# A kernel that picks weights by id: loading W2 for the first batches by id, and b2's rows by GpSimd

## The chip, the cores and the metric

The kernel runs on one core of one Trainium2 chip. A core has a matrix engine (TensorE, PE in the profile; its weight loads are shown as PEld), a vector engine (VectorE, DVE), a scalar engine (ScalarE, ACT), a general engine (GpSimd, POOL) and SyncE (SP), which here issues nearly all transfers. Data lie in HBM, in the on-chip memory SBUF, and in PSUM, eight banks that TensorE writes into. The metric is the device time of one execution in microseconds. The median of three runs of the kernel before is 303.18 us (303.14 to 303.38).

## The reference, cut to what matters

```python
w1 = W1[language_ids]                 # x: (128 batches, 128 rows, 512), ids: (128,)
w2 = W2[language_ids]                 # W1: (10, 512, 128), W2: (10, 128, 512)
h = einsum('bsh,bha->bsa', x, w1) + b1[language_ids][:, None, :]
h = relu(h)
adapted = einsum('bsa,bah->bsh', h, w2) + b2[language_ids][:, None, :]
y = x + adapted
normed = (y - mean(y)) * rsqrt(var(y) + 1e-5)
out = x + normed * gamma[language_ids][:, None, :] + beta[language_ids][:, None, :]
```

Every batch is a tile of 128 rows by 512 columns of fp32 (256 KB), and each uses the weights of its own id, one of ten. One batch's W1 is 256 KB, one batch's W2 is 256 KB, and the tables of all ids are 2.5 MB each.

## The kernel before, in words

For each batch b TensorE does three things: it transposes x in four blocks (`transpose_x`, L271), multiplies the transposed x by the batch's W1 (`down`, L294, eight pieces), and multiplies the result, after ReLU, by the batch's W2 (`up`, L311, two pieces). ScalarE copies the transposed x out of PSUM (`copy_xT`, L275), applies ReLU with b1 (`relu`, L302), sums the squares (`square`, L351) and finds the root (`deviation`, L361). VectorE adds x, or x + b2, to the product and sums the rows (`residual`, L328), subtracts the mean and multiplies by gamma (`scale`, L394), and multiplies by the reciprocal deviation and adds x + beta (`finish`, L403). GpSimd forms x + b2 (`add_b2`, L281) and x + beta (`add_beta`, L288).

For some batches GpSimd does not form x + b2. In `b2_by_matmul` batches a small product on TensorE (L310) adds b2's row into PSUM ahead of `up`; in `b2_by_vector` batches VectorE adds it (`vector_b2`, L321).

The order of the work is written out by hand. The function `keep` ties every instruction to the one issued before it on the same engine, so that each engine works through its list in the order of the program text; across engines, waits follow from the data. The main loop runs over i = 3 to 121 and does in iteration i, with b = i - 3: the transposes of batch i, `down` of i - 1, `up` of i - 2, the vector work of b and of the pair before it, and the additions of GpSimd for b + 2. Before it stands a start written out line by line, after it an end written out likewise. Results leave in pairs of batches (`store`, L407).

Buffers bound how far one engine may run ahead: x in four tiles of four batches (`xp`), the sums x + b2 in four (`rp`), the results in eight pairs (`op`), a batch's W1 in seven (`wp`), products in five PSUM banks (`p_y`).

W2 is held whole in SBUF (`load_w2`, L165; ids 0 to 2 first, 3 to 9 later). `up` picks its id's columns by an address known at run time, so the first `up` waits for all of W2. W1 comes in two ways. For the first `FIRST` = 17 batches `load_first` (L161) loads the id's W1 directly from HBM. For the rest, all of W1 is held in SBUF (`load_w1`, four loads of 640 KB, L103), and `stage_w1` (L262) on ScalarE copies the id's part into the batch's tile. For the same first batches (`EARLY`) the transposes take x in another column order. The end of the kernel loads three more W1 by id.

SP's queue issues, in this order: the ids, gamma's rows, x of batches 0 and 1, W2 of ids 0 to 2, then W1 by id and x of the next batches alternately, W2 of ids 3 to 9 after the fourth W1, the four parts of W1 among batches 13 to 16, and at last x of 18 and 19. Behind these stand the stores and the later loads of x, one megabyte each (`load_x`, L71): stores 0 and 1, x of batches 20 to 23, three stores, x of 24 to 27, and so on. A load by id can be issued only when the ids have arrived and have been clamped by VectorE.

Each row of beta, gamma and b2 (30 rows) is spread over all 128 partitions at the start, in one of two ways: `spread` (L229, L232) multiplies a one-hot column by the rows on TensorE and lets ScalarE copy the product; `shuffle_rows` (L247) lets VectorE copy it out of a tile that holds all rows in each group of 32 partitions (`four_copies`). Before, `spread` does thirteen rows and `shuffle_rows` seventeen. The additions of GpSimd wait for all ten rows of beta, or of b2, since they pick by a run-time address too.

Of the kernel before, what the change touches and what calls it, by code (L numbers as in the profile page):

```python
# [19 lines left out]
FIRST = 17  # L20
EARLY = 17
LATE = 17
U = 2


@with_exitstack
def cond_resid_kernel(ctx: ExitStack, tc: tile.TileContext, x, itok, W1, b1, W2, b2, gamma, beta, out):
# [29 lines left out]
    op = ctx.enter_context(tc.tile_pool(name="op", bufs=8))  # L57
# [31 lines left out]

    warm = const.tile([P, 1], FP, name="warm")  # L90
# [6 lines left out]
    load_part(0, 2)  # L97
    keep(nc.scalar.dma_start(out=b1r, in_=b1))
# [63 lines left out]

    def load_w2(lo, hi):
        dst = w2[:, lo * H : hi * H].rearrange("p (l h) -> p l h", l=hi - lo)
        keep(nc.sync.dma_start(out=dst, in_=W2[lo:hi].rearrange("l a h -> a l h")))  # L165

    load_w2(0, 3)
    load_first(0)
    load_first(1)
    load_part(2, 4)  # L170
    load_first(2)
    load_first(3)
    load_w2(3, L)
    xs[1] = xp.tile([P, G, H], FP, tag="x", name="x_1")
    load_part(4, 6)
    load_first(4)
    load_first(5)
    load_part(6, 8)
    load_first(6)
    load_first(7)  # L180
    xs[2] = xp.tile([P, G, H], FP, tag="x", name="x_2")
    load_part(8, 10)
    load_first(8)
    load_first(9)
    load_part(10, 12)
    load_first(10)
    load_first(11)
    xs[3] = xp.tile([P, G, H], FP, tag="x", name="x_3")
    load_part(12, 14)
    load_first(12)  # L190
    load_w1(0)
    load_first(13)
    load_part(14, 16)
    load_first(14)
    load_w1(1)
    load_first(15)
    xs[4] = xp.tile([P, G, H], FP, tag="x", name="x_4")
    load_part(16, 18)
    load_w1(2)
    load_w1(3)  # L200
    load_first(16)
    load_part(18, 20)
# [20 lines left out]
    b2_b = const.tile([P, L * H], FP, name="b2_b")  # L223

    def spread(r, copier):
# [7 lines left out]
        else:  # L233
            keep(nc.vector.tensor_copy(dst, row))

# [17 lines left out]
    def b2_by_matmul(b):  # L253
        return b in (0, 1) or b >= B - 2

    def b2_by_vector(b):
        return b in (2, 3, 9, 13, 17, 21) or 24 <= b < B - 8 and (b % 16 in (1, 6, 11) or b % 32 == 30)
# [46 lines left out]
    def up(b):  # L304
# [6 lines left out]
        keep(nc.tensor.matmul(ys[b], lhsT=hT[b], rhs=w2[:, bass.ds(v * H, H)], start=not m, stop=True))  # L311
# [230 lines left out]
    spread(10, nc.scalar)  # L542
    spin(1, H)
    x_turn(0)
    transpose_b1()
    spread(11, nc.scalar)
    for n in (0, G):
        lid(n, ET.PE)
    shuffle_rows(0, 10)
    x_turn(1)  # L550
    spread(12, nc.scalar)
    spread(13, nc.scalar)
    down(0)
    relu(0)
    spread(14, nc.scalar)
    x_turn(2)
    spread(15, nc.scalar)
    down(1)
    relu(1)
    spread(16, nc.scalar)  # L560
    spread(17, nc.scalar)
    x_turn(3)
    down(2)
    relu(2)
    spread(18, nc.scalar)
    spread(19, nc.scalar)
    add_beta(0)
    add_beta(1)
    spread(20, nc.scalar)
    spread(21, nc.scalar)  # L570
    down(3)
    relu(3)
    spread(22, nc.scalar)
    add_beta(2)
    add_beta(3)
# [253 lines left out]
```

## Time and profile before

| what | value |
|---|---|
| median of three runs | 303.18 us |
| the profiled execution | 303.08 us, its span 301.3 us |
| TensorE busy | 293.5 us (97%) |
| VectorE busy | 294.0 us (98%) |
| ScalarE busy | 278.5 us (92%) |
| GpSimd busy | 281.0 us (93%) |
| transfers | 78.11 MB, mean 259 GB/s |

The profile is a record of one execution. Its page lists the busy time of each engine, the span in 40 slices with the busy share of engines and of transfers in tenths, the chain of work that ended last, the costliest groups of instructions, and the transfers by the line that issues them. Further views are answers from the same trace: the instructions of one engine in order of time, the busy time and the bytes in chosen stretches, the waits by pairs, and the time from the issue of a load to its landing. Names such as `py<-w,hT` read "written tile <- read tiles"; a row that ends in brackets tells how long the engine was idle before it and what ended that. A busy matrix engine is not one at its peak: its pieces overlap, so the distance between two starts says more than the length of a piece.

### The profile page before, as it was taken

The page shows a single profiled execution, that of the slowest core. Times are in us where ns is not written, and L with a number is a line of the kernel's source. Part 1 is how long each engine was busy: PE and PEld are TensorE (multiplying, and loading weights), DVE is VectorE, ACT ScalarE, POOL GpSimd, SP SyncE. Part 2 cuts the span into 40 slices and gives each one's busy share as a digit, 9 for nine tenths or more (in the row PEclk, how much of TensorE's full clock was granted, in tenths as well). Part 3 has the DMA queues.
Part 4 walks back from the last instruction along what each step waited for, and adds up shares of the span by engine and source line. Part 5 has one row for each costly group of instructions (what it writes and reads, how often), then busy time and mean ns, then how long its engine had stood idle before and what let it go on. Part 6 is the DMA issues. An engine that isn't in the chain of part 4 may idle for free.

```text
span 301.3 us, 7022 instructions
## 1 busy us (share of the span) xinstructions
PE 293.5 (97%) x1827; PEld 219.1 (73%) x1827; DVE 294.0 (98%) x785; ACT 278.5 (92%) x770; POOL 281.0 (93%) x236
## 2 busy tenths in 40 slices
PE   7899999999999999999999999999999999999993
PEld 3758787777777777777777777777777777777761
DVE  6989999999999999999999999999999999999996
ACT  5868789999999999999999999999999999999983
POOL 1299998999999999999999999999999999999982
PEclk9999999999999999999999999999999999999999
DMA  6999999996667776766687666668765767782826
GB/s 234 377 390 367 346 321 396 405 337 209 234 229 256 280 235 197 252 242 233 240 281 250 209 209 246 257 231 281 263 204 196 254 232 253 278 271 79 280 89 228
DMA packets 45353, 78.11 MB, mean 259 GB/s; under 512 B 2137, under 2 KB 9316, under 8 KB 45314
## 3 DMA queue, kind: packets, MB, share of 16 engines
q1 hardware_dynamic: 45254, 77.62, 74.9%
q8 instruction: 15, 0.25, 0.3%
q14 instruction: 24, 0.20, 0.2%
q10 hardware_dynamic: 60, 0.05, 0.1%
HBM read 44.11 MB, written 33.55 MB: 258 GB/s over the span
## 4 chain that ended last, share of the span: by engine, by line
PE 87%; DVE 5%; DMA 3%; issue 2%; SPq 1%; POOL 0%; DVEq 0%; POOLq 0%
PE ph L294 35%; PE py L311 35%; PE pxT L271 18%; DMA w<-in_L_cond_W_dram 3%; DVE py L328 1%; DVE o L488 1%; DVE py L394 1%; SPq L161 1%; DVE n L494 0%; SPq L143 0%; DVE rstd_of L370 0%; SPq L88 0%; DVEq L824 0%; DVE part_of L367 0%; DVE shift L434 0%
## 5 line engine op out<-in xcount | busy, mean ns | idle before, releaser
L288 POOL TENSOR_TENSOR o<-x,beta_b 128x512 f32<-128x512 f32 x121 | 158.4, 1331 | 12.8 <-DVE beta_b L247 11.6
L294 PE MATMUL ph<-xT,w1s 128*128 128x128 f32 x1024 | 135.4, 275 | 0.1
L311 PE MATMUL py<-w,hT 128*128 x256 | 131.5, 595 | 0.6 <-DMA w<-in_L_cond_W_dram 0.6
L294 PEld LDWEIGHTS ph<-xT,w1s 128*128 128x128 f32 x1024 | 124.9, 192 | 1.8 <-issue 0.8
L281 POOL TENSOR_TENSOR r<-x,b_b 128x512 f32<-128x512 f32 x92 | 122.7, 1334 | 0.0
L271 PEld LDWEIGHTS pxT<-ident,x 128*128 128x128 f32 x512 | 65.8, 149 | 66.3 <-issue 49.9
L394 DVE SCALAR_TENSOR_TENSOR py<-py,nmean,gamma_b 128x512 f32<-128x512 f32 x124 | 93.2, 752 | 0.0
L403 DVE SCALAR_TENSOR_TENSOR o<-py,rstd,o 128x512 f32<-128x512 f32 x116 | 86.5, 745 | 0.0
L351 ACT ACTIVATE sq<-py,sum 128x512 f32<-128x512 f32 x124 | 85.8, 692 | 0.2 <-DVE rstd L370 0.2
L275 ACT COPY xT<-pxT 128x512 f32<-128x512 f32 x128 | 74.7, 584 | 5.9 <-PE pxT L271 5.8
L271 PE MATMUL pxT<-ident,x 128*128 128x128 f32 x512 | 77.6, 274 | 0.9 <-ACT gamma_b L232 0.7
L328 DVE SCALAR_TENSOR_TENSOR py<-py,r 128x512 f32<-128x512 f32 x97 | 66.7, 688 | 0.1
L262 ACT COPY w1s<-w 128x512 f32 x108 | 66.2, 613 | 0.0
L302 ACT ACTIVATE hT<-ph,b1T 128x128 f32<-128x128 f32 x128 | 46.9, 367 | 8.6 <-PE ph L294 4.0
L311 PEld LDWEIGHTS py<-w,hT 128*128 128x128 f32 x256 | 39.0, 192 | 2.2 <-DMA w<-in_L_cond_W_dram 1.1
L351 ACT ACTIVATION_READ_ACCUMULATOR sq<-py,sum 128x1 f32 x124 | 25.1, 203 | 0.0
L328 DVE SCALAR_TENSOR_TENSOR py<-py,x 128x512 f32<-128x512 f32 x31 | 21.7, 699 | 0.8 <-PE py L311 0.3
L321 DVE TENSOR_TENSOR py<-py,b_b 128x512 f32<-128x512 f32 x27 | 18.6, 689 | 0.8 <-ACT xT L275 0.6
L361 ACT ACTIVATE root<-ssq,eps 128x2 f32<-128x2 f32 x62 | 16.4, 265 | 0.0
L328 DVE DVE_READ_ACCUMULATOR py<-py,r 128x1 f32 x97 | 13.4, 138 | 0.0
L342 ACT ACTIVATE nmean<-sum 128x2 f32<-128x2 f32 x61 | 12.1, 199 | 0.0
L370 DVE SCALAR_TENSOR_TENSOR rstd<-part,root 128x2 f32<-128x2 f32 x62 | 9.2, 149 | 0.0
(73 smaller groups left out, 104.5 us busy)
## 6 DMA issues: line engine op xcount, KB each, us to landing
out_dram<-o SPq DMA_DIRECT2D x62, 512.0 KB, 3.5
x<-in_x_dram SPq DMA_DIRECT2D x27, 1024.0 KB, 6.5
x<-in_x_dram SPq DMA_DIRECT2D x10, 512.0 KB, 6.0
w1s<-in_L_cond_W_dram SPq DMA_DIRECT2D x20, 256.0 KB, 7.7
w<-in_L_cond_W_dram SPq DMA_DIRECT2D x4, 640.0 KB, 8.4
w<-in_L_cond_W_dram SPq DMA_DIRECT2D x1, 1792.0 KB, 10.2
w<-in_L_cond_W_dram SPq DMA_DIRECT2D x1, 768.0 KB, 5.2
out_dram<-o SPq DMA_DIRECT2D x4, 128.0 KB, 1.7
```

The lines of the kernel that those rows point to most:

```text
L262: keep(nc.scalar.copy(w1s[b].rearrange("p k a -> p (k a)"), src))
L271: keep(nc.tensor.transpose(pxs[b][:, k, :], cols, ident))
L275: keep(nc.scalar.copy(xT[b], pxs.pop(b)))
L281: keep(nc.gpsimd.tensor_tensor(rs[b], xb(b), b2_b[:, bass.ds(v * H, H)], ALU.add))
L288: keep(nc.gpsimd.tensor_tensor(os[g][:, j, :], xb(b), beta_b[:, bass.ds(v * H, H)], ALU.add))
L294: nc.tensor.matmul(phs[b], lhsT=w1s[b][:, k, :], rhs=xT[b][:, k, :], start=(k == 0), stop=(k == KC - 1))
L302: keep(nc.scalar.activation(hT[b], phs.pop(b), AF.Relu, bias=b1T[:, bass.ds(lid(b, ET.Activation), 1)]))
L311: keep(nc.tensor.matmul(ys[b], lhsT=hT[b], rhs=w2[:, bass.ds(v * H, H)], start=not m, stop=True))
L328: nc.vector.scalar_tensor_tensor(ys[b], ys[b], 1.0, r, ALU.mult, ALU.add, accum_out=col(sums, b))
L351: nc.scalar.activation(sq, ys[b], AF.Square, bias=col(sums, b), scale=-float(H), accum_out=col(ssqs, b))
L394: nc.vector.scalar_tensor_tensor(ys[b], ys[b], col(nmeans, b), gamma_b[:, bass.ds(v * H, H)], ALU.add, ALU.mult)
L403: nc.vector.scalar_tensor_tensor(o, ys[b], rstds[g][:, j : j + 1], o, ALU.mult, ALU.add)
```

## The change

The transfers at the start are put into a new order. W2 of the first five batches is loaded by id into tiles taken from the result buffers (`load_early`), that of batch 0 as the first load by id; all of W2 comes later, in one load, behind x of batch 7. x of batches 2 to 9 comes batch by batch. W1 is loaded by id for eighteen batches instead of seventeen, and its last two parts stand behind x of 19. The load of batches 20 to 23 stands behind one store instead of two. b2 (20 KB) is loaded once more, as one row, by ScalarE's queue, and GpSimd spreads it over the partitions in two instructions. Of beta and gamma seven rows are spread by TensorE and thirteen shuffled by VectorE, in another order, and `up` of batch 0 now stands ahead of `down` of batch 3. b2 goes in by TensorE for batches 0, 1, 2 and 4, by VectorE for 3, 5, 8, 15, 17 and 23 among the first 24. There are nine output buffers instead of eight. The main loop's arithmetic stays the same.

```diff
-FIRST = 17
-EARLY = 17
-LATE = 17
+FIRST = 18
+EARLY = 18
+LATE = 18
+SOON = 5
...
-    op = ctx.enter_context(tc.tile_pool(name="op", bufs=8))
+    op = ctx.enter_context(tc.tile_pool(name="op", bufs=9))
...
+    keep(nc.scalar.dma_start(out=b2_b[0:1, :], in_=b2.rearrange("(o l) h -> o (l h)", o=1)))
...
+    def early_w2(b):
+        if b // 2 not in soon:
+            soon[b // 2] = op.tile([P, 2, H], FP, tag="o", name=f"soon_{b // 2}")
+        return soon[b // 2][:, b % 2, :]
+
+    def load_early(b):
+        src = W2[bass.ds(lid(b, ET.SP), 1)].rearrange("o a h -> a (o h)")
+        keep(nc.sync.dma_start(out=early_w2(b), in_=src))
...
-    load_w2(0, 3)
+    load_early(0)
     load_first(0)
+    load_part(2, 3)
+    load_early(1)
+    load_part(3, 4)
+    load_early(2)
     load_first(1)
-    load_part(2, 4)
     load_first(2)
     load_first(3)
-    load_w2(3, L)
...
-    load_part(4, 6)
+    load_part(4, 5)
     load_first(4)
     load_first(5)
-    load_part(6, 8)
+    load_early(3)
+    load_part(5, 6)
     load_first(6)
+    load_early(4)
+    load_part(6, 7)
     load_first(7)
+    load_part(7, 8)
+    load_w2(0, 10)
...
     load_part(16, 18)
+    load_w1(1)
+    load_part(18, 20)
+    load_first(16)
     load_w1(2)
     load_w1(3)
-    load_first(16)
-    load_part(18, 20)
+    load_first(17)
...
+    for half in range(2):
+        cols = slice(half * (L // 2) * H, (half + 1) * (L // 2) * H)
+        keep(nc.gpsimd.partition_broadcast(b2_b[:, cols], b2_b[0:1, cols]))
...
-        return b in (0, 1) or b >= B - 2
+        return b in (0, 1, 2, 4) or b >= B - 2
...
-        return b in (2, 3, 9, 13, 17, 21) or 24 <= b < B - 8 and (b % 16 in (1, 6, 11) or b % 32 == 30)
+        return b in (3, 5, 8, 15, 17, 23) or 24 <= b < B - 8 and (b % 16 in (1, 6, 11) or b % 32 == 30)
...
+        rhs = early_w2(b) if b < SOON else w2[:, bass.ds(v * H, H)]
+        keep(nc.tensor.matmul(ys[b], lhsT=hT[b], rhs=rhs, start=not m, stop=True))
...
-        if b == 8 or b > 12 and b % G == 2 and b // G + 3 < NG:
-            load_x(5 if b == 8 else b // G + 3)
-        up_to = i
+        if b == 6 or b > 12 and b % G == 2 and b // G + 3 < NG:
+            load_x(5 if b == 6 else b // G + 3)
+        up_to = 5 if i == 4 else i
```

The new start, between the first row spread and the main loop, reads:

```python
    spread(4, nc.scalar)
    x_turn(0)
...
    spin(1, H)
    x_turn(1)
    spread(18, nc.scalar)
...
    down(0)
    relu(0)
    x_turn(2)
    down(1)
    relu(1)
    spread(5, nc.scalar)
    spread(6, nc.scalar)
    shuffle_rows(2, 3)
    down(2)
    relu(2)
    x_turn(3)
...
    spread(1, nc.scalar)
    up(0)
    down(3)
    relu(3)
...
    spread(7, nc.scalar)
    x_turn(4)
    add_beta(0)
    add_beta(1)
...
    add_beta(2)
    up(1)
    add_beta(3)
```

63 lines of the change are left out of this document (31 added, 32 removed).

## The prediction

> **What bounds the kernel now.** I read the page first (busy times, the slices, the chain), then the order of time of TensorE, then the waits, then the loads.
>
> ```profile
> span 301.3 us, 7022 instructions
> PE 293.5 (97%) x1827; PEld 219.1 (73%) x1827; DVE 294.0 (98%) x785; ACT 278.5 (92%) x770; POOL 281.0 (93%) x236
> DMA  6999999996667776766687666668765767782826
> PE 87%; DVE 5%; DMA 3%; issue 2%; SPq 1%; POOL 0%; DVEq 0%; POOLq 0%
> PE ph L294 35%; PE py L311 35%; PE pxT L271 18%; DMA w<-in_L_cond_W_dram 3%; DVE py L328 1%; DVE o L488 1%; DVE py L394 1%; SPq L161 1%; DVE n L494 0%; SPq L143 0%; DVE rstd_of L370 0%; SPq L88 0%; DVEq L824 0%; DVE part_of L367 0%; DVE shift L434 0%
> ```
>
> All four engines are nearly full, but the chain is TensorE's: three groups of its matmuls make 88% of the span, and the only transfer in it is a load of W2 at the start. The DMA row matters as much: the transfer engines are full for the first nine of 40 slices (68 us), then half idle. A change of loads acts there.
>
> The order of time of TensorE (start, length, line, operation, what ended the idle time):
>
> ```profile
> 16.43 1.12 PE L311 MATMUL py<-w,hT 128*128 x2 [0.58 <-DMA w<-in_L_cond_W_dram]
> 22.17 0.63 PE L271 MATMUL pxT<-ident,x 128*128 128x128 f32 x4
> 25.75 1.02 PE L311 MATMUL py<-w,hT 128*128 x2
> 26.61 0.63 PE L271 MATMUL pxT<-ident,x 128*128 128x128 f32 x4
> 48.78 0.60 PE L271 MATMUL pxT<-ident,x 128*128 128x128 f32 x4
> 49.22 1.06 PE L294 MATMUL ph<-xT,w1s 128*128 128x128 f32 x8
> 50.97 0.60 PE L271 MATMUL pxT<-ident,x 128*128 128x128 f32 x4
> 53.16 0.60 PE L271 MATMUL pxT<-ident,x 128*128 128x128 f32 x4
> 279.21 0.60 PE L271 MATMUL pxT<-ident,x 128*128 128x128 f32 x4
> ```
>
> The rows of L271 are the transposes of batches 6 (22.17), 8 (26.61), 18 (48.78), 19 (50.97), 20 (53.16) and 123 (279.21). From 48.78 to 279.21 lie 105 batches: 2.19 us each. Two neighbours give 2.19 too, so TensorE goes back to back in a fixed pitch and never catches up. Whatever its position is at batch 20 or so is carried to the end, as long as the others follow. The kernel's time is therefore decided in the first 55 us: by TensorE's own work there, and by the loads that it waits for. The row at 16.43 is the start's only wait on a load: up(0) on the second W2 load.
>
> **The loads.** TensorE's three kinds of input come over SP's queue in the order in which they are issued. Columns below: stretch, its length, busy times, clock, DMA share, GB/s; then issues of SP, and time to landing of four of them (the load of W2's last seven ids at 6.22, W1 of batch 4 at 7.86, W1 of batch 16 at 37.63, the second store at 41.55).
>
> ```profile
> 0.00:4.00 4.00, 2.99 (x7) 0.88 (x7) 2.49 (x11) 1.91 (x3) 0.88 (x8) 1.00 0.33 110
> 4.00:16.00 12.00, 10.28 (x66) 7.57 (x65) 10.97 (x33) 9.92 (x22) 2.90 (x3) 1.00 1.03 378
> 16.00:24.00 8.00, 7.57 (x39) 5.01 (x40) 6.83 (x20) 5.24 (x17) 8.00 (x7) 1.00 1.05 388
> 24.00:32.00 8.00, 8.00 (x53) 6.35 (x52) 8.00 (x22) 6.50 (x20) 8.00 (x8) 1.00 1.09 359
> 32.00:40.00 8.00, 8.00 (x51) 6.11 (x50) 7.83 (x22) 6.48 (x19) 8.00 (x7) 1.00 1.12 334
> 40.00:48.00 8.00, 8.00 (x56) 6.53 (x55) 8.00 (x22) 6.50 (x20) 6.83 (x7) 1.00 1.09 350
> 48.00:52.00 4.00, 4.00 (x27) 2.95 (x27) 4.00 (x14) 3.91 (x12) 4.00 (x4) 1.00 1.05 398
> ...
> 1.52 0.41 SPq L88 DMA_DIRECT2D x<-in_x_dram  x1
> 1.98 0.47 SPq L165 DMA_DIRECT2D w<-in_L_cond_W_dram  x1
> 3.75 0.91 SPq L161 DMA_DIRECT2D w1s<-in_L_cond_W_dram  x2
> 37.63 2.82 SPq L161 DMA_DIRECT2D w1s<-in_L_cond_W_dram  x1
> 41.03 0.92 SPq L407 DMA_DIRECT2D out_dram<-o  x2
> 42.05 1.33 SPq L71 DMA_DIRECT2D x<-in_x_dram  x1
> ...
> DMA to landing us min/median/max: 10.2/10.2/10.2
> DMA to landing us min/median/max: 10.6/10.6/10.6
> DMA to landing us min/median/max: 7.1/7.1/7.1
> ```
>
> The share is above 1 from 4 us on: the engines have no gap to take more. Summing GB/s times length, the bytes moved stand at 0.44 MB at 4 us, 4.98 at 16, 8.08 at 24, 10.95 at 32, 13.62 at 40, 16.42 at 48, 18.01 at 52. I count the queue in units of 256 KB (0.262 MB: one batch's x, W1 or W2) and add 0.09 MB of rows. W2's second load ends at 18 units of queue, 4.8 MB: moved at 15.5, landed at 6.22 + 10.2 = 16.4, a lag of 0.9. Batch 4's W1: 5.6 MB, 17.5, landed 18.5, lag 1.0. Batch 16's W1 (55 units): 14.5 MB, 42.5, landed 44.7, lag 2.2. The second store (61 units): 16.1 MB, 47.1, landed 48.6 (the third row's 7.1 holds for both), lag 1.5. So a transfer lands when its place in the queue has been moved, plus 0.9 early, plus about 1.6 (0.9 to 2.2) later.
>
> **The change part by part.**
>
> *TensorE's start.* Thirteen row spreads become seven, two more b2 products are added (batches 2 and 4), up(0) needs only its own 256 KB. In the order of time, two adjacent pieces start 0.21 apart:
>
> ```profile
> 4.99 0.38 PE L229 MATMUL row<-parts,pick 96*128 96x512 bf16 x1
> 5.21 0.38 PE L529 MATMUL idle<-ones 128*128 128x512 bf16 x1
> 10.04 0.72 PE L271 MATMUL pxT<-ident,x 128*128 128x128 f32 x4 [0.71 <-ACT gamma_b L232]
> ```
>
> Six spreads less save 1.3, two products cost 0.4; the waits of 0.58 (W2) and 0.71 (a copy of a spread row) can go. Sum before batch 8: up to -2.1 us. VectorE (17 shuffled rows become 13) and ScalarE (13 copies become 7) get lighter and hide behind TensorE; ScalarE's one more DMA issue (about as long as SP's above, 0.4 us) stands ahead of its first work and is covered by the wait for batch 1's W1, now seventh of the units behind x0 and x1.
>
> *The same start by the loads.* The queue has now, ahead of the whole W2 load's end, x of batches 0 to 7 (8 units), early W2 (5), W1 of 0 to 7 (8), W2 (10): 31 units, 8.2 MB. By the stretches that is moved at 24.4. Before, W2's first load at 1.98 fed the engines until W1 could be addressed at 3.75; now nothing stands between x (0.61 MB with the rows, moved at about 4.45) and that 3.75. From x's issue at 1.52 to bytes in number (0.44 MB by 4 us) I estimate 1 us of latency, so bytes again from 4.75: 0.3 later. Landed: 24.4 + 0.3 + 0.9 = 25.6. up(5), the first product to need it, stood at 25.75. So of the 2.1 us hardly 0.1 is left at batch 5: the load of W2 takes the place of the work. Late next is x of batch 20.
>
> *The loads behind it.* Up to the end of load_x(5) (batches 20 to 23, one 1 MB load) the queue held 65 units, 17.1 MB: moved at 48 + (17.1 - 16.42)/0.398 = 49.8, landed with the lag of 1.6 at 51.4; TensorE wanted it at 53.16, 1.8 later. After: five W2 units and one W1 unit more, one store (2 units) less ahead of it: 4 units, 1.05 MB, and 0.02 for b2's row. At the 398 GB/s of that stretch 2.7 us (3.2 at 334). Landing: 51.4 + 2.7 + 0.3 = 54.4, TensorE's place 53.16: 1.2 us late. The second place says the same: W1 of batch 17 now comes from HBM behind all of W1, at 63 units, 16.6 MB, moved at 48.5, landed at 48.5 + 0.3 + 1.6 = 50.4; down(17) stood at 49.22: also 1.2. These two are one shift, not two: a TensorE that is 1.2 late at 17 meets batch 20's x in time. load_x(6) follows with one store less between: no later place is tight, since from 68 us on the engines have room.
>
> *ScalarE's W1 copy* moves from batch 17 to 18, one copy of 0.61 us less, and the pitch later; it waits for all of W1, which lands one unit ahead of batch 17's W1, about 49.7, where the copy would stand at 46.20 + 2.19 = 48.4. The wait falls into the same shift.
>
> ```profile
> 46.20 0.61 ACT L262 COPY w1s<-w 128x512 f32 x1
> ```
>
> *GpSimd.* It had no idle time but these two, and its result is used with a lead:
>
> ```profile
> 13.10 4.98 POOL L288 TENSOR_TENSOR o<-x,beta_b 128x512 f32<-128x512 f32 x4 [11.64 <-DVE beta_b L247]
> 18.03 1.28 POOL L281 TENSOR_TENSOR r<-x,b_b 128x512 f32<-128x512 f32 x1
> 47.58 2.51 POOL L288 TENSOR_TENSOR o<-x,beta_b 128x512 f32<-128x512 f32 x2 [1.17 <-DMA out_dram<-o]
> 209.01 1.38 POOL L281 TENSOR_TENSOR r<-x,b_b 128x512 f32<-128x512 f32 x1
> 213.67 0.68 DVE L328 SCALAR_TENSOR_TENSOR py<-py,r 128x512 f32<-128x512 f32 x1
> ```
>
> The smallest lead that I found: the sum done at 210.39, read at 213.67, 3.3 us. The trace has no partition broadcast. From below: four additions go in 4.93 us, so 1.23 for 512 columns is the engine's two-input pace; a one-input write could be three times as fast, 4 us for 5120 columns; from above: that pace itself, 12.3 us. From b2's row at about 4 us it ends at 8 to 16; I take 12, the middle, since neither row is nearer. The first addition waits also for the last beta row, which ScalarE now copies after relu(3): by TensorE's order about 16. So it starts at 16 instead of 13.1; two b2 additions less give 2.5 back: 0.4 behind before, with 3.3 of lead. Cost 0. If the cover goes, it costs what exceeds a start at 13.1 + 2.5 + 3.3 = 18.9. The ninth output buffer moves the wait of 1.17 to batch 18, where store 0, also about 4 us later, lets it stand at about 0.6: 0. A shift of TensorE by 1.2 adds as much lead.
>
> The Trainium skill, GPSIMD Engine Reference, section Instruction dispatch, says that the first call to a freshly loaded kernel pays about 6 us that no instruction shows. If the broadcast is such a call, by that estimate its range of ends becomes 14 to 22, of which only the upper part passes 18.9; no run here shows it yet.
>
> Sum on the profiled execution's 303.08 (span 301.3 and 1.8 around it; the median of the runs, 303.18, is 0.1 above): TensorE's work -2.1, taken back by W2's landing +2.0, then the later loads +1.3: **304.3 us**. Its own range is 303.4 (lag 0.9) to 305.8 (lag 2.2, 3.2 us for the units).
>
> **The rivals.**
> *The loads are hidden anyway.* Batch 20's x had 1.8 us to spare; if the lag shrinks to 0.9 because smaller transfers keep the 16 engines closer together, landing is 53.7 less what the engines gain, and TensorE stays within 0.5 of its old place: 303.2. For it: the lag of early loads. Against it: shares above 1 throughout.
> *Faster.* W2 lands a microsecond earlier than the sum (24.6), as it would if the 31 units went at the best stretch's 398 GB/s from 4.75 on with a lag below 0.9, and batch 17's W1 and batch 20's x follow as early: TensorE keeps 1.1 of its 2.1 and the time is 302.0. It decides from landings under 48.6 and 52.5 there. Against it: 1.05 MB more has to go through a full queue. The whole 2.1 (301.0) would need W2 by 23.6, when 8.2 MB have not been moved.
> *GpSimd becomes the bound.* A broadcast that ends at 21 starts the additions 2.1 past 18.9; its row of idle times shows no gap in which it could catch up: 305.2, at 24 us 308. For it: no row of this operation exists here; against: the rows' bounds end at 16. By the Trainium skill's rule above the upper bound would be 22.
> *The early batches alone do not gain,* W2's landing slipping to 26.5 with a lag as later: 303.8, then the same late loads. This is in the first case's range.
>
> **How the numbers follow.** The late loads, 0.55; hidden, 0.22; faster, 0.15; GpSimd, 0.08. The likeliest gives 304.3. A measurement of this kernel can tell about 0.2% (0.6 us) from no change. Faster by that: 0.15. Slower: GpSimd's 0.08 and of the late loads all but their lowest part, 0.51: 0.59. Within: 0.26. The range leaves out the lower half of the faster case and the tails of GpSimd's and of the late loads: 302.1 to 305.6.
>
> **What would show it.** Right: the waits of TensorE name W2 at L338 near 25 to 26, and near 49 to 54 W1 of batch 17 or x, 1 us or more; the transposes of batch 20 begin at 54.4, from there the pitch is 2.19; additions on GpSimd begin near 16. Wrong: batch 20's transposes before 52.6 (the queue moved more than 400 GB/s, or the lag fell), a wait of VectorE for GpSimd (broadcast too long), or a pitch other than 2.19 after 60 us, which would make the start no measure of the end.

## The result, and the profile after

The changed kernel takes 311.88 us (median; 310.98 to 313.05), the kernel before 303.28 us on the same chip (303.14 to 303.40): a ratio of 1.0292, 95% interval 1.0275 to 1.0310. It is slower by 8.6 us; 304.3 was forecast, with a range to 305.6. The profiled execution took 310.98 us, its span 309.2 us, 7.9 us over the span of 301.3 before.

The page of the changed kernel: span, busy time of two engines, the share of the transfer engines by slice, the chain of work that ended last.

```profile
span 309.2 us, 7035 instructions
PE 295.9 (96%) x1823; PEld 220.9 (71%) x1823; DVE 291.5 (94%) x777; ACT 275.9 (89%) x763; POOL 284.2 (92%) x236
DMA  5999999998766766886767667887667668872825
PE 72%; DVE 13%; issue 7%; DMA 5%; SPq 1%; DVEq 1%; POOL 0%; POOLq 0%
```

TensorE has four matmuls fewer, and 2.4 us more busy time (1.7 of it by the half clock below); VectorE and ScalarE have less work. Most of the 7.9 us lies in waits. TensorE in order of time, changed kernel (start, length, line, operation, idle time before it and what ended that):

```profile
12.73 1.13 PE L320 MATMUL ph<-xT,w1s 128*128 128x128 f32 x8 [2.35 <-DMA w1s<-in_L_cond_W_dram]
16.23 1.02 PE L338 MATMUL py<-soon,hT 128*128 128x512 f32 x2
28.74 1.10 PE L338 MATMUL py<-w,hT 128*128 x2 [1.73 <-DVE o L430]
29.68 0.63 PE L297 MATMUL pxT<-ident,x 128*128 128x128 f32 x4
51.88 0.60 PE L297 MATMUL pxT<-ident,x 128*128 128x128 f32 x4
58.72 0.63 PE L297 MATMUL pxT<-ident,x 128*128 128x128 f32 x4 [2.30 <-DMA x<-in_x_dram]
59.18 1.57 PE L320 MATMUL ph<-xT,w1s 128*128 128x128 f32 x8
60.55 1.91 PE L338 MATMUL py<-w,hT 128*128 x2
62.25 0.95 PE L297 MATMUL pxT<-ident,x 128*128 128x128 f32 x4
227.22 0.60 PE L297 MATMUL pxT<-ident,x 128*128 128x128 f32 x4
```

The rows of L297 are the transposes of batches 8 (29.68), 18 (51.88), 20 (58.72), 21 (62.25) and 96 (227.22). Before, batches 8, 18 and 20 began at 26.61, 48.78 and 53.16: the lateness is 3.07, 3.10 and 5.56. Batches 21 and 22 add the rest, to 7.25, and from there it stands: 7.29 at batch 96 by the row at 219.93 below. The first step is the product of batch 5 at 28.74. The row puts its wait down to VectorE, but the trace's record of W2's one load shows its last part landed at 28.61, and in x5_parts below, which has the same start, the same product began at 27.23, right behind W2's landing at 27.09 and ahead of the same VectorE instruction, which it therefore does not need. The second is the x of batch 20. The third is not a wait: behind 58.72 the pieces are half as long again. The stretches (length, busy times, granted clock, share of the transfer engines, GB/s), changed kernel:

```profile
4.00:6.00 2.00, 1.16 (x4) 0.60 (x4) 1.06 (x2) 0.93 (x2) 0.00 (x0) 1.00 0.52 184
6.00:11.00 5.00, 4.38 (x25) 3.23 (x23) 4.17 (x14) 3.53 (x7) 2.60 (x1) 1.00 1.00 313
48.00:52.00 4.00, 4.00 (x27) 3.00 (x26) 3.88 (x10) 3.28 (x10) 4.00 (x4) 1.00 1.04 314
52.00:56.00 4.00, 4.00 (x29) 3.06 (x27) 3.94 (x11) 3.84 (x13) 4.00 (x5) 1.00 0.90 307
56.00:59.56 3.56, 1.26 (x9) 0.87 (x9) 3.56 (x10) 1.40 (x5) 3.56 (x3) 1.00 1.04 403
59.56:62.97 3.41, 3.41 (x13) 2.26 (x12) 0.50 (x2) 2.26 (x7) 3.41 (x4) 0.50 1.05 407
```

In the last row the clock is 0.50 for 3.41 us, which costs 1.7 us. The first two rows matter against the same stretches of the kernel before:

```profile
4.00:6.00 2.00, 1.40 (x9) 0.94 (x8) 1.25 (x2) 1.28 (x3) 0.00 (x0) 1.00 1.04 354
6.00:11.00 5.00, 4.03 (x25) 2.83 (x25) 4.72 (x17) 3.63 (x8) 0.00 (x0) 1.00 1.03 382
```

By 11 us the changed kernel has moved 2 x 170 + 5 x 69 = 685 KB less, 1.8 us of transfers at the 382 GB/s of the last row.

GpSimd, changed kernel, in order of time, and then the instructions of its lines L260 and L314 (length in ns min/median/max, first and last start):

```profile
8.40 5.48 POOL L260 PARTITION_BROADCAST b_b<-b_b  x2 [6.71 <-issue]
22.58 7.42 POOL L314 TENSOR_TENSOR o<-x,beta_b 128x512 f32<-128x512 f32 x6 [8.70 <-ACT nmean L369]
292.74 2.51 POOL L450 TENSOR_TENSOR o<-x,beta_b 128x512 f32<-128x512 f32 x2
```

```profile
L260 POOLq MODIFY_POOL_CONFIG  x2: 11/11/11, 1.7 to 1.7; - x2
...
L314 POOLq MODIFY_POOL_CONFIG  x2: 127/127/127, 13.8 to 13.8; - x2
```

GpSimd is told to change its configuration at 1.7, the broadcast begins 6.7 us later; it is told to change back at 13.8, and the first addition begins 8.8 us later, at 22.58 instead of 13.10. Of the 9.5 us in between, a part is the new order of the start: ScalarE's copy of the last beta row now ends at 19.02 (begun at 18.44, 0.58 long). From the kernel before, as the mark for the far end of the run, TensorE's transposes of batch 96 and GpSimd's last pair of beta additions:

```profile
219.93 0.60 PE L271 MATMUL pxT<-ident,x 128*128 128x128 f32 x4
```

```profile
286.66 2.61 POOL L423 TENSOR_TENSOR o<-x,beta_b 128x512 f32<-128x512 f32 x2
```

So at the far end TensorE is 7.29 us late and GpSimd 292.74 - 286.66 = 6.08 us. In this profiled execution, the fastest of the four, TensorE is the later of the two, and the chain of the page names GpSimd with 0%. The other three executions have no profile.

### The profile page after: what moved, and what is told of

Same layout as the page of the kernel before. It is cut to its first block, busy times and chain, and to the rows that moved or that the text cites. A ratio compares the mean times of both kernels' runs of the same rounds, so it can differ in the third digit from the quotient of the medians.

```text
span 309.2 us, 7035 instructions
## 1 busy us (share of the span) xinstructions
PE 295.9 (96%) x1823; PEld 220.9 (71%) x1823; DVE 291.5 (94%) x777; ACT 275.9 (89%) x763; POOL 284.2 (92%) x236
## 4 chain that ended last, share of the span: by engine, by line
PE 72%; DVE 13%; issue 7%; DMA 5%; SPq 1%; DVEq 1%; POOL 0%; POOLq 0%
PE ph L320 29%; PE py L338 28%; PE pxT L297 14%; DVE py L355 4%; DVE py L421 4%; DMA x<-in_x_dram 3%; DMA w1s<-in_L_cond_W_dram 2%; DVE o L430 2%; DVE o L515 1%; DVE py L348 1%; DVE part L394 0%; DVE n L521 0%; SPq L175 0%; DVE part L392 0%; PE row L251 0%
## 5 line engine op out<-in xcount | busy, mean ns | idle before, releaser
L314 POOL TENSOR_TENSOR o<-x,beta_b 128x512 f32<-128x512 f32 x121 | 155.6, 1302 | 8.7 <-ACT nmean L369 8.7
L338 PE MATMUL py<-w,hT 128*128 x246 | 127.3, 599 | 1.7 <-DVE o L430 1.7
L307 POOL TENSOR_TENSOR r<-x,b_b 128x512 f32<-128x512 f32 x90 | 117.6, 1306 | 0.0
L297 PEld LDWEIGHTS pxT<-ident,x 128*128 128x128 f32 x512 | 66.7, 150 | 67.8 <-issue 53.0
L297 PE MATMUL pxT<-ident,x 128*128 128x128 f32 x512 | 78.6, 277 | 2.3 <-DMA x<-in_x_dram 2.3
L355 DVE SCALAR_TENSOR_TENSOR py<-py,r 128x512 f32<-128x512 f32 x95 | 65.5, 690 | 3.9 <-PE py L338 3.3
L338 PEld LDWEIGHTS py<-w,hT 128*128 128x128 f32 x246 | 37.6, 193 | 2.7 <-DVE o L430 1.9
L355 DVE SCALAR_TENSOR_TENSOR py<-py,x 128x512 f32<-128x512 f32 x33 | 23.0, 698 | 5.5 <-PE py L338 1.9
L260 POOL PARTITION_BROADCAST b_b<-b_b x2 | 5.5, 2800 | 6.7 <-issue 6.7
```

What stands on the lines that cost most here:

```text
L297: keep(nc.tensor.transpose(pxs[b][:, k, :], cols, ident))
L307: keep(nc.gpsimd.tensor_tensor(rs[b], xb(b), b2_b[:, bass.ds(v * H, H)], ALU.add))
L314: keep(nc.gpsimd.tensor_tensor(os[g][:, j, :], xb(b), beta_b[:, bass.ds(v * H, H)], ALU.add))
L338: keep(nc.tensor.matmul(ys[b], lhsT=hT[b], rhs=rhs, start=not m, stop=True))
L355: nc.vector.scalar_tensor_tensor(ys[b], ys[b], 1.0, r, ALU.mult, ALU.add, accum_out=col(sums, b))
```

## The experiments

Two questions: which parts cost the 8.6 us, and whether the two delays, TensorE's and GpSimd's, add or run in parallel. The table is for all runs. "Late" is the start of the mark in the run's profile less that of the mark before (219.93 and 286.66); "over before" is the median less that of the kernel before on the same chip (303.28 in the first row, 302.94 in the last, 302.87 to 303.12 in the others). The marks are those of one execution, the median that of four (six in the last row).

| kernel | median | over before | first addition | TensorE late | GpSimd late |
|---|---|---|---|---|---|
| changed kernel | 311.88 | 8.6 | 22.58 | 7.29 | 6.08 |
| no_broadcast | 307.47 | 4.6 | 17.98 | 4.03 | 2.07 |
| only_broadcast | 314.10 | 11.2 | 25.41 | 7.70 | 11.19 |
| x5_parts | 311.90 | 9.0 | 24.76 | 5.35 | 8.24 |
| spin_20 | 310.29 | 7.4 | 25.41 | 7.53 | 8.70 |
| tiny_broadcast | 309.07 | 6.0 | 21.42 | 3.71 | 6.57 |
| pool_late | 311.03 | 7.9 | 21.79 | 4.04 | 7.44 |
| gap_filled | 305.48 | 2.4 | 18.15 | 3.08 | 1.60 |
| spin_w2 | 307.18 | 4.1 | 17.97 | 3.27 | 1.52 |
| loads_mended | 304.88 | 2.0 | 18.02 | 2.32 | 1.37 |
| loads_mended_pool | 311.38 | 8.5 | 24.84 | 5.49 | 8.20 |
| pool_relieved | 307.69 | 4.8 | 26.65 | 4.73 | 3.94 |
| pool_late_2 | 304.33 | 1.4 | 16.73 | -0.10 | 2.42 |

### The two halves of the change: no_broadcast and only_broadcast

no_broadcast is the changed kernel without the GpSimd part:

```diff
-    keep(nc.scalar.dma_start(out=b2_b[0:1, :], in_=b2.rearrange("(o l) h -> o (l h)", o=1)))
...
-        keep(nc.gpsimd.partition_broadcast(b2_b[:, cols], b2_b[0:1, cols]))
...
     x_turn(2)
+    spread(20, nc.scalar)   # and 21, 22
     down(1)
...
     shuffle_rows(14, 15)
+    shuffle_rows(23, 25)    # 25 to 27 after residual(0), 28 and 29 after residual(1)
```

> The changed kernel without its GpSimd part: b2's ten rows are spread again, three by TensorE and ScalarE, seven by VectorE, and neither b2's row load nor the broadcast is there. Theory 'the loads': the loss (8 us) comes from W2's last piece at 28.6 us, batch 20's x at 58.6 and half a clock for 3.4 us behind that wait; the GpSimd part costs nothing on the path. Then this runs in 311 to 312.5 us, TensorE's product of batch 5 begins at 28.2 to 29, and only GpSimd's first addition moves, from 22.6 to about 19. Rival 'GpSimd': the broadcast and the code that it has loaded slow the transfers (2 KB pieces of 0.6 to 0.9 us between 7 and 10 us) or hold the additions back. Then the product of batch 5 begins 1 us or more earlier and the time is 310.5 or less.

only_broadcast is the kernel before with that part alone:

```diff
     load_part(0, 2)
+    keep(nc.scalar.dma_start(out=b2_b[0:1, :], in_=b2.rearrange("(o l) h -> o (l h)", o=1)))
...
+        keep(nc.gpsimd.partition_broadcast(b2_b[:, cols], b2_b[0:1, cols]))
...
-    spread(20, nc.scalar)   # and 21, 22
...
-    shuffle_rows(23, 30)
```

> The kernel before with the GpSimd part alone: b2's row load and the broadcast in place of the three spread and seven shuffled rows. Theory 'the loads': three row spreads less save up to 0.65 us of TensorE ahead of up(0), which then waits as much longer for W2; GpSimd's first addition goes from 13.1 to about 22, and its lead of 3.3 us over VectorE is used up: the time stays within 303 to 304. Rival 'GpSimd': additions that begin at 22 in a kernel whose VectorE asks for them 2 to 3 us earlier than in the changed one make VectorE wait: 305 to 309.

Measured: 307.47 us (ratio 1.0145, 1.0113 to 1.0178) and 314.10 us (1.0364, 1.0344 to 1.0384). The theory that I held after reading the trace, that the loads are the whole cause, fell twice: the GpSimd part is worth 4.0 us in the changed kernel (8.6 less 4.6) and 11.2 us alone. What is left without it, 4.6 us, is more than the prediction's 1.2 for TensorE's start and the loads together. TensorE and VectorE of only_broadcast:

```profile
33.74 1.12 PE L316 MATMUL py<-w,hT 128*128 x2 [3.75 <-DVE part L372]
```

```profile
26.70 0.75 DVE L408 SCALAR_TENSOR_TENSOR o<-py,rstd,o 128x512 f32<-128x512 f32 x1 [1.43 <-POOL o L293]
31.60 0.70 DVE L333 SCALAR_TENSOR_TENSOR py<-py,r 128x512 f32<-128x512 f32 x1 [4.15 <-POOL r L286]
```

VectorE waits for GpSimd's sums and TensorE for VectorE, which has to free the PSUM banks. In no_broadcast the wait for W2 is shown under its own name, and a half clock of 3.41 us follows it:

```profile
27.91 1.10 PE L333 MATMUL py<-w,hT 128*128 x2 [2.02 <-DMA w<-in_L_cond_W_dram]
```

```profile
29.11:32.52 3.41, 3.41 (x14) 2.63 (x13) 2.77 (x7) 1.69 (x6) 3.41 (x3) 0.50 1.05 386
```

The halves do not add (4.6 + 11.2 is not 8.6), so they run in parallel at least in part.

### What in the GpSimd part costs: tiny_broadcast, pool_late, pool_late_2

tiny_broadcast leaves the kernel before as it is and broadcasts two columns of a scratch tile:

```diff
+    tiny = const.tile([P, 2], FP, name="tiny")
+    keep(nc.gpsimd.memset(tiny, 0.0))
+    keep(nc.gpsimd.partition_broadcast(tiny, tiny[0:1, :]))
```

> The kernel before, unchanged but for one partition broadcast of two columns of a scratch tile on GpSimd, before its additions; b2's rows are spread as before. Theory 'code changes': GpSimd changes its code ahead of the broadcast (6.7 to 9.2 us in the runs so far) and again ahead of the first addition (8.7 to 11.4 us), whatever the size: the first addition begins at 17 to 20 us instead of 13.1, GpSimd, which has no idle time to catch up, carries it to the end, where its lead is 1.35 us (from the three runs with the broadcast: end after the kernel before's = lateness - 1.35): 302.9 + 2.6 to 5.6 = 305.5 to 308.5. Rival 'the broadcast's own work': 5.5 us of it for all ten rows, nothing for two columns: additions at 13.1 to 14.5, time 302.8 to 303.3.

pool_late has no broadcast, but six additions more ahead of the first:

```diff
+    late = rp.tile([P, H], FP, tag="r", name="late")
+    for _ in range(6):
+        keep(nc.gpsimd.tensor_tensor(late, xb(0), beta_b[:, bass.ds(lid(0, ET.Pool) * H, H)], ALU.add))
     add_beta(0)
```

> The kernel before with six additions more on GpSimd (into a scratch tile that nothing reads) ahead of the first one: 6 x 1.23 = 7.4 us more, and no change of code. Theory: GpSimd's lateness goes to the end less 1.35 us of lead in the last batches: 302.9 + 6.0 = 308.9 (308.4 to 309.4). Rival 1, the lead of 3.3 us that the prediction took from the row at 210 us: 307.0. Rival 2, GpSimd catches up in its waits for stores (1.2 us in all): 305 or less. If the time is 308.9, the 11 us of the broadcast in the kernel before are the lateness of its additions (12.3 us) and nothing of its port or of its transfers.

Measured: 309.07 us (1.0202, 1.0180 to 1.0225) and 311.03 us (1.0265, 1.0246 to 1.0285). GpSimd of tiny_broadcast:

```profile
10.34 0.26 POOL L238 PARTITION_BROADCAST tiny<-tiny  x1 [8.61 <-issue]
21.42 4.96 POOL L292 TENSOR_TENSOR o<-x,beta_b 128x512 f32<-128x512 f32 x4 [10.82 <-DMA w1s<-in_L_cond_W_dram]
293.23 2.51 POOL L427 TENSOR_TENSOR o<-x,beta_b 128x512 f32<-128x512 f32 x2
```

The broadcast of two columns is 0.26 us long and costs 6 us. What costs is the change to it and back (8.6 and 10.8 us), not the spreading; 8.3 us of it show in the first addition, since GpSimd had nothing to add before 13.10 anyway. The release named in the second row, a load of W1, is not the cause: in the kernel before the same addition began at 13.10. pool_late shows that a late first addition (21.79) has such a price without any broadcast. It came out 2 us above its expectation: in its profile the clock is 0.50 for 3.41 us near the end (1.7 us), and the six additions took 1.34 us each (from 13.78 to 21.79) instead of 1.23. So the third run asks for the threshold, with two additions in place of six:

> The kernel before with two additions more on GpSimd ahead of its first one, into a scratch tile that nothing reads. Theory 'the last batches have no lead': the first addition begins 3.1 to 3.4 us later, the one wait for a store takes 1.2 back, and 2.0 of lateness less 0.2 to 0.7 comes to the end: 304.2 to 304.9. Rival, the lead of 3.3 us that the prediction took from the row at 210 us: hidden, 302.8 to 303.3.

Measured: 304.33 us (1.0039, 1.0026 to 1.0053). Three views of this run: GpSimd, TensorE, VectorE.

```profile
16.73 4.99 POOL L288 TENSOR_TENSOR o<-x,beta_b 128x512 f32<-128x512 f32 x4
...
289.08 2.55 POOL L423 TENSOR_TENSOR o<-x,beta_b 128x512 f32<-128x512 f32 x2
```

```profile
219.83 0.60 PE L271 MATMUL pxT<-ident,x 128*128 128x128 f32 x4
```

```profile
285.51 0.70 DVE L328 SCALAR_TENSOR_TENSOR py<-py,r 128x512 f32<-128x512 f32 x1 [0.95 <-POOL r L427]
287.98 0.70 DVE L328 SCALAR_TENSOR_TENSOR py<-py,r 128x512 f32<-128x512 f32 x1 [0.70 <-POOL r L427]
```

This run separates the main loop from the end. GpSimd begins 3.63 us late and, one wait for a store later (1.2), stays 2.4 us late for 270 us. TensorE is on time at batch 96, as a lead of 3.3 us would have it. And then, in the last batches, VectorE waits twice for GpSimd, 1.65 us in all, and the span ends at 303.1, 1.8 us later. The lead of the main loop does not exist in the end written out by hand. The six executions fall into two groups, three at 303.72 to 303.84 us and three at 304.81 to 304.82; the profile is of the upper one, and the lower one is still 0.9 us over the kernel before. What parts them is open.

### The loads: gap_filled, spin_w2, loads_mended

All three are without the GpSimd part. gap_filled loads x of batches 2 and 3, which needs no id, while SP waits for the ids:

```diff
+    load_part(2, 4)
     load_early(0)
     load_first(0)
-    load_part(2, 3)
     load_early(1)
-    load_part(3, 4)
     load_early(2)
```

> The changed kernel without its GpSimd part (b2 spread), and x of batches 2 and 3 as one load right behind x of 0 and 1, ahead of the loads by id: they need no id, and fill the time from 1.98 to 3.78 us in which SP waits for the ids. Theory 'W2's landing sets batch 8': the queue loses 0.9 us less at its start, W2 lands at 26.7 to 27.0 instead of 27.8, TensorE's wait for it falls from 2.0 to about 1.1 us, and the time from 307.5 to 305.5 to 306.7 (less than that where the half clock behind the wait is rarer). Rival: the by-id loads of batches 0 and 1 land 1 us later and TensorE waits there instead; the place of batch 8 and the time stay (307 to 308).

spin_w2 fills the wait for W2 on TensorE (products into the bank of `down`, overwritten later):

```diff
+        if i - U == 5:
+            idle5 = p_h.tile([P, P], FP, tag="h", name="idle5")
+            for _ in range(28):
+                keep(nc.tensor.matmul(idle5, lhsT=ones, rhs=ones[:, 0:1].to_broadcast([P, P]), start=True, stop=True))
         if i - U >= 2 and on(i - U):
             up(i - U)
```

> The changed kernel without its GpSimd part, and 28 idle products (128 columns, 0.056 us each, 1.6 us) on TensorE ahead of batch 5's up product, where it waits 2.0 us for W2. Theory 'idle time halves the clock': the wait is filled but for 0.5 us, the 3.4 us at half clock, which the profiled run without this had at 29.1 us, do not come, and the time goes from 307.5 (306.4 to 308.5) to 305.8 to 306.6, with less spread. Rival: half clocks as often as before, 307.3 to 307.8.

loads_mended has the gap filled, and batch 20's x as a load of its own:

```diff
-            load_x(5 if b == 6 else b // G + 3)
+            if b == 6:
+                xs[5] = xp.tile([P, G, H], FP, tag="x", name="x_5")
+                load_part(20, 21)
+                load_part(21, 24)
+            else:
+                load_x(b // G + 3)
```

> The changed kernel without its GpSimd part, with x of batches 2 and 3 in the gap ahead of the loads by id, and batch 20's x as a load of its own ahead of 21 to 23. Theory 'two lateness in parallel, TensorE's by W2 and batch 20's x, GpSimd's by its first addition, the later one sets the end': TensorE is 1.1 us late at batch 8 as with the gap filled, batch 20's x adds 0.5 or less instead of 1.4 to 1.9, GpSimd is 1.5 us late as before: 304.0 to 304.9. Rival: the wait for x goes to batch 21 or a later group: 305.2 to 305.8, as with the gap filled alone.

Measured: gap_filled 305.48 us (1.0076, 1.0059 to 1.0093), spin_w2 307.18 us (1.0160, 1.0117 to 1.0203), loads_mended 304.88 us (1.0058, 1.0042 to 1.0075). TensorE of gap_filled and of loads_mended:

```profile
26.78 1.10 PE L332 MATMUL py<-w,hT 128*128 x2 [0.73 <-DMA w<-in_L_cond_W_dram]
55.83 0.63 PE L291 MATMUL pxT<-ident,x 128*128 128x128 f32 x4 [1.19 <-DMA x<-in_x_dram]
```

```profile
27.03 1.10 PE L332 MATMUL py<-w,hT 128*128 x2 [1.11 <-DMA w<-in_L_cond_W_dram]
```

Two units of x in the gap bring the first product that needs all of W2 forward from 27.91 to 26.78, and the time over the kernel before falls from 4.6 to 2.4 us. Half clocks, which two of no_broadcast's four executions show by their mean clock, may be a part of that. Then batch 20's x is late next, and its own small load takes that wait away: the second row has no counterpart in loads_mended, where that x landed at 52.31 and its transposes began at 54.56. The gain in time is only 0.4 to 0.6 us, since TensorE loses 0.7 again at batch 24. Of what is left, 1.1 to 1.4 us stand at batch 8, behind W2. spin_w2 settles nothing about the clock: no half clock in its profile up to the end, 2 of its 4 executions with a mean clock under 0.995, as many as without the products (2 of 4).

### At batch 20 with the GpSimd part in place: x5_parts and spin_20

x5_parts is the changed kernel with the second edit of loads_mended alone; spin_20 has ten idle products ahead of batch 20's transposes:

```diff
+        if b == 20:
+            for _ in range(10):
+                keep(nc.tensor.matmul(pxs[b].rearrange("p k s -> p (k s)"), lhsT=ones, rhs=ones[:, 0:1].to_broadcast([P, H]), start=True, stop=True))
         for k in range(KC):
```

> The changed kernel with the load of batches 20 to 23 in two parts, batch 20 alone first (256 KB), then the other three. Theory 'the loads': batch 20's x lands some 2 us earlier, TensorE's wait of 2.3 us before its transposes falls under 0.7, the half clock behind it (3.4 us at 0.5, 1.7 us) does not come, and the time is 308 to 309.5. Rival 'the place in the queue does not decide': one ring of the sixteen is 2 to 3 us behind the others there, a quarter of the load waits for the same ring, and the time stays at 311 to 312.5. Third: the wait goes to batch 21 (the three quarters land as late as the whole): 310.5 to 311.5.

> The changed kernel with ten idle products on TensorE (0.22 us each, into the bank that batch 20's transposes then overwrite) ahead of batch 20's transposes, where it waited 2.3 us for x. Theory 'idle time halves the clock': with the wait filled the clock stays at 1.00 through 59 to 63 us, the transposes begin at the same 58.7, and the time is 1.5 to 2 us under the changed kernel's: 309.5 to 310.5. Rival 'the clock falls for another reason': still 0.5 for 3.4 us, time unchanged or 0.2 above.

Measured: 311.90 us (1.0300, 1.0282 to 1.0317) and 310.29 us (1.0236, 1.0217 to 1.0254). x5_parts missed its 308 to 309.5 although the load did what was expected: no wait for x at batch 20, TensorE 5.35 late instead of 7.29. A part of that is not the edit's: W2, which comes before it, landed 1.5 us earlier in this profile than in the changed kernel's (27.09 instead of 28.61):

```profile
27.23 1.10 PE L338 MATMUL py<-w,hT 128*128 x2 [0.55 <-DMA w<-in_L_cond_W_dram]
```

GpSimd's additions began at 24.76 in this run and it is 8.24 us late: the end is GpSimd's, and a TensorE that is 1.9 us better buys nothing. spin_20 is not a test in the end: TensorE was held up by W2 (2.14 us) and, through VectorE, by GpSimd (1.49) before it came to batch 20, never waited there, and the ten products cost it 2.2 us.

### Both together: loads_mended_pool and pool_relieved

loads_mended_pool is the changed kernel with the two edits of loads_mended; pool_relieved takes five additions off GpSimd besides:

```diff
-        return b in (0, 1, 2, 4) or b >= B - 2
+        return b in (0, 1, 2, 4, 6, 7, 9, 10, 11) or b >= B - 2
```

> The same two mends of the loads in the changed kernel with its GpSimd part. Theory 'two lateness in parallel': GpSimd's first addition still begins at 22.5 to 25.5 us, so GpSimd is 6 to 9 us late from there to the end, and the end is late by that less 0.2 to 0.7: 308.5 to 311.6, although TensorE's own loads cost only 1.5 us. Rival 'the loads are the cause': 304.5 to 306, near the kernel without the GpSimd part.

> The kernel just described, and b2 of batches 6, 7, 9, 10 and 11 by TensorE instead of GpSimd: five additions of 1.23 us less on GpSimd, five products of 0.22 us more on TensorE. Theory: GpSimd's lateness falls by 6.2 us to 0 to 2.7, TensorE's rises by 1.1 us to 2.5 to 3, and the time is 305 to 306.5, some 4 us under the run with the mends alone. Rival 'the broadcast slows transfers or other engines by its port': the time stays above 308.

Measured: 311.38 us (1.0276, 1.0252 to 1.0301) and 307.69 us (1.0156, 1.0119 to 1.0192). loads_mended_pool: GpSimd, VectorE, and the chain of its page.

```profile
24.84 6.20 POOL L313 TENSOR_TENSOR o<-x,beta_b 128x512 f32<-128x512 f32 x5 [8.92 <-ACT hT L327]
...
294.86 2.64 POOL L449 TENSOR_TENSOR o<-x,beta_b 128x512 f32<-128x512 f32 x2
```

```profile
33.53 0.70 DVE L354 SCALAR_TENSOR_TENSOR py<-py,r 128x512 f32<-128x512 f32 x1 [1.91 <-POOL r L306]
...
291.39 0.70 DVE L354 SCALAR_TENSOR_TENSOR py<-py,r 128x512 f32<-128x512 f32 x1 [1.25 <-POOL r L453]
```

```profile
PE 69%; POOL 10%; DMA 8%; DVE 6%; issue 5%; POOLq 1%; DVEq 0%; SPq 0%
```

With the loads mended the changed kernel still needs 311.4 us, and the same kernel without the GpSimd part 304.9: 6.5 us for the part, and GpSimd now stands in the chain (0% before). Taking five additions off GpSimd gives 3.7 us back. It missed its range by 1.2 us. Here the first addition began at 26.65, and VectorE's finish of batch 0 waited for it, and TensorE for VectorE (2.72 us at batch 5, the largest wait in its profile):

```profile
27.94 0.75 DVE L429 SCALAR_TENSOR_TENSOR o<-py,rstd,o 128x512 f32<-128x512 f32 x1 [2.98 <-POOL o L313]
```

No version of the changed kernel beats the kernel before; loads_mended, the best, is 2.0 us above it.

## Why the prediction was wrong

Two terms of the sum failed, and either alone would have carried the time out of the range. The cost of GpSimd, put at 0, left out a mechanism: with the loads mended, the GpSimd part alone still costs 6.5 us (311.4 against 304.9). The loads and TensorE's start, together +1.2, had the mechanism right and the size wrong: 4.6 us without the GpSimd part. The two run side by side, and the later one sets the end, so they do not add. That the loads would make the kernel slower was forecast; how far, and that GpSimd would, was not.

**TensorE is the pace, and its place at batch 20 is carried to the end.** Right as far as it goes: 7.25 at batch 22, 7.29 at batch 96. What the step left out is that GpSimd does the same. It too has no idle time after the start, and its lateness at the far end follows from its first addition alone: 9.48 late in the changed kernel, less 1.2 (the wait for a store) and 2.5 (two additions fewer), makes 5.8; 6.08 measured. The end follows the later of two engines: TensorE's lateness plus 0.0 to 0.6, or GpSimd's less 0.2 to 0.7 where the half clock does not add to it (in pool_late it does).

**The start's work, -2.1.** Too large. Ahead of batch 7's transposes lie the same `down` and `up` in both orders. Before, they began at 24.39; in the changed kernel at 25.48 with the 2.35 us of wait for W1 behind them, so without it 1.26 earlier; in no_broadcast at 24.37, with 0.56 us of wait and three row spreads more (0.65), which makes 1.23. (The transposes of batch 4, 1.4 us earlier in no_broadcast, are no measure: `up` of batch 1 stood ahead of them before and stands behind them now.) Of the 0.85 us that are missing, I put 0.7 down to TensorE's clock, as an estimate: the trace's record of the granted clock has 1.00 from 8.36 us on in the changed kernel and from 4.41 before, and the first two groups of transposes took 1.06 and 1.04 us instead of 0.63 and 0.75.

**The wait for batch 1's W1.** Forecast as a cover and not as a loss; it was 2.35 us. It cost nothing by itself, since W2 took its place: no_broadcast, with 0.56 us of wait there, is 2.24 us late at batch 8.

**W2's landing, 25.6.** Measured 28.61; at batch 8 TensorE is 3.07 late where -0.1 was forecast (-2.1 and +2.0). The idle stretch of the queue was priced at 0.3 and was 170 KB x 2 (0.9 us), then five slow microseconds (313 instead of 382 GB/s, 0.9 us), which no step foresaw; together 1.8. The lag was 0.9 in the forecast. The trace keeps sixteen completions for a load, one by each transfer engine, and they show why it was more:

```
load                          kernel before: median, 15th, last   changed: median, 15th, last
W2 (ids 3-9 / all ids)        15.99  16.28  16.39                  26.47  27.39  28.61
x of batches 20 to 23         50.24  51.00  51.17                  55.60  56.66  58.58
```

One engine of the sixteen was 2.1 us behind the median at W2 and 3.0 us behind at batch 20's x, where 0.4 and 0.9 stood before.

The kernel before has such lags too, only not at these two loads: its loads that landed from 24.3 to 42.1 us had their last part 1.5 to 1.9 behind the median. A 16 KB packet of instructions, 1.1 us long, fits W2's. It was moved at 21.67 before and at 23.63 in the changed kernel. From the last load that landed before the packet was through to the first one after it, the lag goes from 0.42 to 1.53 before, and from 1.04 to 2.14 in the changed kernel: 1.1 us, the packet's length, both times. W2 landed ahead of the packet before, and behind it now. In x5_parts, with the same start, the packet came only at 30.85; there W2's last part was 0.55 behind and landed at 27.09. In the eleven other profiles the lag grows by 0.5 to 1.6 at the first such packet, but in x5_parts it stays near 1.0 there. So the packet fits W2's lag and is not shown as its cause; no run moved it on purpose. The 3.0 us at batch 20's x are not explained by it: over the next packet, at 46.12, the lag stays at 1.9 to 2.0, and grows only behind 53.3 us.

**The later loads, 50.4 and 54.4.** Batch 17's W1 landed at 52.08, x of 20 to 23 at 58.58 instead of 54.4. Of the 4.2 us beyond the forecast, 1.5 are the start's (1.8 where 0.3 was counted) and 2.1 the last engine's (3.0 behind the median, 0.9 before). That leaves 0.6, while the slower stretch from 48 to 56 us (314 and 307 GB/s where 398 was used) would by itself make 1.8 (0.70 MB less in 8 us, at 398), so the shares overlap and the split is an estimate. The step named the right load; it wanted "1.2 us late", and TensorE, though 3.1 us late already, waited 2.30. gap_filled, with TensorE 1.3 late at that place, waited 1.19.

**GpSimd, cost 0: the step whose mechanism failed.** The end of the broadcast, forecast at 12, was 13.9, not far off; the last beta row, forecast at 16, held the first addition until 17.98 in no_broadcast. Two things in it were wrong. The change back to additions, 8.8 to 11.5 us from its instruction to the first addition in the seven profiles with a broadcast, was not counted at all: it puts the first addition at 22.6 to 26.7 instead of 18 in the kernels with the changed start. And the lead of 3.3 us is that of the main loop; the last batches have 0.2 to 0.7. The trace of the kernel before shows it, some 75 us behind the rows from which the 3.3 was taken:

```profile
284.20 2.62 POOL L427 TENSOR_TENSOR r<-x,b_b 128x512 f32<-128x512 f32 x2
```

```profile
286.26 0.69 DVE L328 SCALAR_TENSOR_TENSOR py<-py,r 128x512 f32<-128x512 f32 x1
```

The first of these two sums, 1.39 us long, is done at 285.59 and is read at 286.26: a lead of 0.7. The place from which a late start costs is therefore not 18.9 but 13.1 + 1.2 + 2.5 + 0.5 = 17.3, and the first addition at 22.58 is worth 5.3 us where the rival's formula gives 3.7. The rival "GpSimd becomes the bound" was the case with a chance of 0.08.

The Trainium skill, GPSIMD Engine Reference, section Instruction dispatch, counts about 6 us for the first call to freshly loaded code, with no instruction shown. The trace agrees in kind and shows more than 6: 6.7 to 9.2 us to the first broadcast, and 8.8 to 11.5 us again at the way back, with instructions that mark both. I had used the rule for one change only.

**The half clock.** In no step. In the changed kernel's profile it follows the wait of 2.30 us and is worth 1.7 of the 7.29. Of thirteen waits of TensorE of 1.7 us or more in the profiles of this study four were followed by it (2.30 here, 2.02 in no_broadcast, 3.75 in only_broadcast, 1.91 near the end of pool_late), nine not, the 2.35 at 12.73 and pool_late's 2.19 at 30 us among them. The Trainium skill, TensorE: Matmul & The Clock Gate, section What's actually happening, has the clock set by a window of 3413 ns that runs freely. The trace's record of the granted clock agrees: its stretches are 51.20, 3.41 and 245.76 us long in the changed kernel, 15, 1 and 72 times 3.413, and in all fourteen profiles each stretch that ends within the kernel is a whole multiple. The changes lie on a grid, which starts elsewhere in each execution (first change at 8.36 here, 8.63 in no_broadcast, 4.36 in only_broadcast). On that grid it is not the length of a wait that tells, but how long TensorE was busy in one stretch of 3.41 us:

| profile, stretch | wait of TensorE in or across it | TensorE busy, us of 3.41 | clock in the next stretch |
|---|---|---|---|
| changed kernel, 56.14 to 59.56 | 2.30 | 1.12 | 0.50 |
| only_broadcast, 31.67 to 35.08 | 3.75 | 1.33 | 0.50 |
| no_broadcast, 25.70 to 29.11 | 2.02 | 1.39 | 0.50 |
| pool_late, 291.51 to 294.92 | 1.91 | 1.49 | 0.50 |
| spin_20, 25.94 to 29.35 | 2.14 | 1.54 | 1.00 |
| x5_parts, 292.70 to 296.12 | 1.84 | 1.58 | 1.00 |
| changed kernel, 25.42 to 28.83 | 1.73 | 1.68 | 1.00 |
| pool_late, 28.68 to 32.09 | 2.19 | 1.92 | 1.00 |

Behind the first full clock, no stretch with 1.54 us or more was followed by the half clock in any of the profiles, and each with 1.39 or less was; between them one went each way (1.49 above, and 1.46 at the very end of spin_w2, followed by 1.00). So the same wait counts or not by where it falls on the grid. These are readings of traces; no run set the stretch on purpose.

**The rivals "hidden" and "faster"** needed landings that did not come. The pitch of 2.19 us behind 62 us, the waits of TensorE at W2, and the wait for x were as forecast in place, and too small in size.

## What to carry to other kernels

Before work is moved to an engine that has no idle time, look at its first use in the whole program and at its lead in the last batches: lateness of a full engine travels to the end, and the smallest lead there counts, not that of the main loop. An operation of a kind that the engine does not run elsewhere in the kernel has to be priced with the change to it and the change back. Where two engines are both full, mend them together or the mend shows nothing (x5_parts: TensorE 1.9 us better, time the same).

## What was not expected of the hardware

A partition broadcast of 2560 columns takes 2.80 us on GpSimd (5.48 for two), one of two columns 0.26, but the change to it and back took 15.5 to 19.5 us together, with GpSimd idle, and differed between kernels with the same start (first addition at 22.58, 24.76 and 25.41). TensorE runs at half its clock for 3.41 us behind a stretch of 3.41 us in which it was busy for less than some 1.5, on a grid that a wait of 1.9 us can meet or miss. And a load is as late as the last of sixteen transfer engines: up to 3.0 us behind the median of them in the changed kernel, against at most 1.9 before.
